# A four-batch vision layer pair on one core: square roots through ln and exp, normalization on ScalarE, weighted sums on TensorE, last stores on another queue

## The chip, the core and the metric

The kernel runs on one core of a Trainium2 chip. The core has five engines with a queue each: PE (TensorE, matrix products), DVE (VectorE), ACT (ScalarE), POOL (GpSimd) and SP (SyncE, which here only issues DMAs). Each engine takes its instructions strictly in the order of its queue; engines wait for each other through semaphores. An instruction that waits holds everything behind it on its engine.

The metric is the device time of one execution in microseconds (us). Before the change it is 4483.56 us, the median of three runs (4473.93 to 4485.39).

## The reference

Input x is 4 batches of 384 channels by 32 x 32 pixels, that is, 1024 tokens of 384 values per batch, all float32. Two layers follow each other:

```
x = x + L0_conv(ln_c(x))        # selective scan in four directions, then layernorm and gelu
t = tokens(x)
t = t + L0_ffn(ln_t(t))         # mixture of 4 experts, the best 2 per token, weighted
x = x + L1_conv(ln_c(x))        # attention, 8 heads of 64, keys = queries = values
t = t + L1_ffn(ln_t(t))         # a feed-forward layer with Kronecker weights, gelu

def _ln_c(v, eps=1e-6):
    return (v - mean(v)) / sqrt(var(v) + eps)

# the experts' part:
probs = softmax(x @ gate_w + gate_b); keep the two largest, divide by their sum -> masked
y_e = gelu(x @ w1[e] + b1[e]) @ w2[e] + b2[e]
out = sum over e of masked[e] * y_e

# the scan's step size, and the scan itself, for each channel and 16 states:
dt = softplus(...) ; h = h * exp(dt * A) + dt * u * B ; y = sum(h * C)
```

Every normalization needs 1/sqrt(var + eps). Each token's result of the expert stage is a sum of two experts' rows, each times a gate weight.

## The kernel before, in words

**Two strands.** The scan (`scan_layer`) takes the four batches one after the other. The tail of a batch (experts, attention, feed-forward) runs beside the scan of the next batches: the tail of batch b-1 is emitted after the scan of batch b in the program, but a planner, which simulates a time for every instruction, sets the order of each engine's queue. Instructions of route, combine, prologue and last_layers have a higher priority. What stands in a queue is therefore the planner's order, and a change of one instruction's cost or engine reorders many others.

**The scan.** A batch has 4 directions x 2 halves of 512 positions x 3 groups of 128 channels = 24 blocks, here called chunks; four batches have 96. A chunk (`chunk`) takes 16 blocks of exp, scan and product: ACT makes `da` = exp(dt * A) (L429) into one of two PSUM buffers; POOL makes `bx` (L420) in one of six buffers; DVE scans (L434, into `bx` or in place into `da`) and multiplies half of the results by C (L441), POOL the other half (L448); PE sums over the states (L455, `acc`), which frees `bx`; DVE adds `acc` to `y` (L282, L286). One chunk ahead, `project` computes dt: ACT's Abs, Relu, Exp (L351), Identity (L352), Ln (L353), Identity, and then DVE's L383 and a copy L384; the result goes to DRAM and comes back spread over partitions (`dtr<-dd`).

**Roots.** `layernorm` (two halves per call; `start` before a batch's scan and `finish` after it) squares on ACT, sums with PE into `ln_var`, takes Sqrt (L178), and a reciprocal on DVE (L180). `stats` (in `prologue` and in `last_layers`) and `spread` (in `route`) do the same with bn_stats, Sqrt (L525, L636) and reciprocal. ACT holds one table set at a time. `exp_again` (L144) puts a load of the set `natural_log_exp_and_others` behind every Sqrt and every Gelu. Where an activation's function is not in the set that is active at its place in the queue, the compiler puts a load ahead of it.

**Experts.** `route` sorts the tokens by expert: it normalizes rows on DVE (L649) and scatters them with 16 indirect DMAs from POOL (L654). `experts` runs 11 slots: xs is gathered, transposed, multiplied by w1 (L879, `h_ps`), bias on ACT (L884), Gelu (L888), multiplied by w2 (L895, `y_ps`), bias added by DVE (L899), and stored to `made` by SP's queue (L900).

**Combine and prologue.** When the last slot is stored, `combine` loads the tokens into `xt`, gathers each token's two rows into `got` (16 indirect DMAs from POOL, L913), scales each by its gate on ACT into PSUM (L920), adds them to `xt` on DVE (L924), and stores `xt` through SP (L925). `prologue` takes the stats of `xt`, normalizes it in place on DVE (`normalize`, L531, which has to wait for that store), transposes with PE (L939, `tc_ps`) and copies with ACT (L943, `xc`). Attention starts with products of `xc` (L964, `w_ps`), then `s_ps` (L987), `ex` (L992), `o_acc` (L1036). `last_layers` is L1083 to L1156, with Gelu at L1128.

route(b+1) is emitted between attention(b) and last_layers(b), so the experts of batch b+1 follow the attention of batch b. The last batch is routed after the scan's end in a larger pool of buffers (`WIDE`).

**Buffers that the change touches.** `k4` (4 KB per partition: 5 buffers, 4 in WIDE) holds xs, xc, y, ex and others; `kw` (8, or 10 in WIDE) holds expert weights, then `got`, then attention's `w`, `vt` and `att`; `w_ps` is two PSUM banks.

Of the kernel before, what the change touches and what calls it, by code (L numbers as in the profile page):

```python
# [12 lines left out]
ALU = mybir.AluOpType  # L13
# [4 lines left out]
P = 128  # L18
# [96 lines left out]
class Body:  # L115
# [29 lines left out]

    def col(self, name, i):
        at = COL[name][0] + i
        return self.cols[:, at : at + 1]

    def layernorm(self, src, dst, eps, psum, work):  # L150

        nc = self.nc
        for i in range(NH):
# [16 lines left out]
            for m in range(nm):  # L170
# [6 lines left out]
            self.exp_again(  # L177
                nc.scalar.activation(std, var[:, :nm], AF.Sqrt, bias=eps, scale=1.0 / D).ins  # L178
            )
            nc.vector.reciprocal(std, std)  # L180
# [304 lines left out]
    def first_layer(self, b, room):  # L485

        self.experts(b, self.slots, room)
        with self.tc.high_priority(offset=FORWARD):
            xt = self.combine(b, *self.place, room)
            return self.prologue(xt, xt, room)  # L490
# [25 lines left out]
    def stats(self, xt, eps, room):  # L516
# [8 lines left out]
        self.exp_again(nc.scalar.activation(rstd, mv[:, :, 1], AF.Sqrt, bias=eps).ins)  # L525
        nc.vector.reciprocal(rstd, rstd)
        return mv[:, :, 0], rstd

    def normalize(self, xt, mean, rstd, out):
        for m in range(MB):  # L530
            self.nc.vector.tensor_scalar(  # L531
                out[:, m, :], xt[:, m, :], mean[:, m : m + 1], rstd[:, m : m + 1],
                op0=ALU.subtract, op1=ALU.mult,
            )
# [71 lines left out]
    def spread(self, b, x1, room):  # L606
# [29 lines left out]
        self.exp_again(nc.scalar.activation(rstd, mv[:, :, 1], AF.Sqrt, bias=self.eps5).ins)  # L636
        nc.vector.reciprocal(rstd, rstd)
        nc.vector.tensor_mul(sc, sc, rstd.unsqueeze(2).to_broadcast([P, MB, NE]))
        nc.vector.tensor_add(sc, sc, self.bg.unsqueeze(1).to_broadcast([P, MB, NE]))
        pos, gate, expert = self.places(sc, room)  # L640
# [4 lines left out]
        for m in range(MB):  # L645
            if m % 2 == 0:
                xt = room.tile([P, 2, D], "k4", "xt")
                nc.sync.dma_start(out=xt, in_=self.tokens(b)[:, m : m + 2, :])
            nc.vector.tensor_scalar(  # L649
                xt[:, m % 2, :], xt[:, m % 2, :], mv[:, m, :1], rstd[:, m : m + 1],  # L650
                op0=ALU.subtract, op1=ALU.mult,
# [155 lines left out]
    def experts(self, b, routed, room):  # L807
# [57 lines left out]
        for s in range(NSLOT):  # L865
# [34 lines left out]
            nc.sync.dma_start(  # L900
# [29 lines left out]
    def prologue(self, xt, xn, room):  # L930

        nc = self.nc
# [453 lines left out]
```

## Time and profile before

| What | us |
|---|---|
| median of three runs | 4483.56 |
| the profiled execution's own time | 4517.48 |
| its span | 4513.6 |
| PE busy | 3440.6 (76%) |
| POOL busy | 3037.0 (67%) |
| DVE busy | 3010.8 (67%) |
| ACT busy | 2534.3 (56%) |
| ACT table loads, 185 of 1283 ns | 237.3 |
| mean granted TensorE clock | 0.831 |

The profile is one execution on the chip. In the lines shown below, "L420" is line 420 of the program, "PEld" the weight loads of PE, and `out<-in` names buffers. A group line gives the engine, the operation, the shapes and the count, then the busy time in us, the mean in ns of one, the idle time of the engine just before these instructions, and what ended that idle time. A line of stretches gives start and end, the length, the busy us of each engine with the count of instructions, the granted clock of PE, the DMA engines' mean busy share and the GB/s. A line of waits names who waited for whom, the total in us, how many times, and the longest. A line of the chain gives a start, a length and what the end of the kernel was waiting for.

PE splits each float32 product into two recorded matmuls, so 912 products of y_ps appear as 1824.

### The profile page before, as it was taken

What the parts mean: (1) busy time and instruction counts of PE and PEld (TensorE: products, weight loads), DVE (VectorE), ACT (ScalarE), POOL (GpSimd) and SP (SyncE); (2) the same over time, 40 slices, a digit from 0 to 9 for tenths busy, and PEclk for the clock granted to TensorE, in tenths of its full rate; (3) what the DMA queues carried; (4) which work ended last, traced back from release to release, by engine and by line L of the source; (5) the groups of instructions that cost most, each with busy time, mean ns of one, the idle gap of its engine ahead of it and who ended that gap; (6) DMA issues with size and microseconds to landing.
All of it is one profiled execution on the core that took longest, in us unless ns stands there. A gap on an engine that the chain in (4) does not pass through costs nothing. (4 is left out here: it accounts for less than half of the span.)

```text
span 4513.6 us, 46925 instructions
## 1 busy us (share of the span) xinstructions
PE 3440.6 (76%) x13852; PEld 1652.0 (37%) x13852; DVE 3010.8 (67%) x4344; ACT 2534.3 (56%) x4406; POOL 3037.0 (67%) x1467
## 2 busy tenths in 40 slices
PE   6545554479894787669998588757998689999796
PEld 2111121145552222225555222214555445556333
DVE  4999997878878977977877777896778520002102
ACT  4555554456665676466666577556666444334554
POOL 4999998788987877778988778878889510000100
PEclk7666665589996898669998699858999789999897
DMA  4444554477886533457779443445787543344200
GB/s 119 118 123 118 146 136 106 137 230 209 231 240 181 149 84 104 130 159 226 210 220 275 137 114 101 115 139 170 232 244 232 169 157 115 107 127 153 75 16 15
DMA packets 404361, 684.81 MB, mean 152 GB/s; under 512 B 50944, under 2 KB 206464, under 8 KB 404096
## 3 DMA queue, kind: packets, MB, share of 16 engines
q1 hardware_dynamic: 395360, 656.16, 50.3%
q0 software_dynamic: 8192, 25.17, 1.7%
q8 instruction: 111, 1.82, 0.2%
q14 instruction: 154, 1.26, 0.1%
q10 hardware_dynamic: 544, 0.40, 0.0%
HBM read 561.47 MB, written 120.06 MB: 151 GB/s over the span
## 5 line engine op out<-in xcount | busy, mean ns | idle before, releaser
L420 POOL TENSOR_TENSOR bx<-dtr,bcs 128x1024 f32<-128x1024 f32 x768 | 1797.8, 2366 | 227.7 <-PE acc L455 103.5
L429 ACT ACTIVATE da<-dtr,nega 128x512 f32<-128x512 f32 x1536 | 1045.5, 691 | 1039.4 <-DVE bx L441 569.0
L448 POOL TENSOR_TENSOR bx<-bx,bcs 128x1024 f32<-128x1024 f32 x384 | 903.6, 2358 | 211.8 <-DVE bx L434 88.0
L455 PE MATMUL acc<-bx,sel 128*32 128x512 f32 x3072 | 511.8, 713 | 312.4 <-POOL bx L448 248.8
L879 PE MATMUL h_ps<-xc,w 128*128 128x256 f32 (+1 forms) x3168 | 680.1, 370 | 61.7 <-DVE xc L861 31.5
L895 PE MATMUL y_ps<-w,hs 128*128 128x384 f32 x1824 | 649.9, 509 | 49.8 <-ACT hs L888 44.1
L879 PEld LDWEIGHTS h_ps<-xc,w 128*128 128x128 f32 x3168 | 557.2, 200 | 253.4 <-issue 120.4
L434 DVE TENSOR_TENSOR_SCAN bx<-da,carry,bx 128x512 f32<-128x512 f32 x384 | 474.0, 1269 | 118.6 <-POOL bx L420 65.5
L434 DVE TENSOR_TENSOR_SCAN bx<-da,bx 128x512 f32<-128x512 f32 x384 | 452.2, 1209 | 129.2 <-POOL bx L420 70.3
L434 DVE TENSOR_TENSOR_SCAN da<-da,carry,bx 128x512 f32<-128x512 f32 x384 | 476.5, 1273 | 67.9 <-ACT da L429 62.6
L441 DVE TENSOR_TENSOR bx<-da,bcs 128x512 f32<-128x512 f32 x768 | 509.8, 679 | 3.8
L434 DVE TENSOR_TENSOR_SCAN da<-da,bx 128x512 f32<-128x512 f32 x384 | 456.3, 1218 | 60.7 <-ACT da L429 44.2
L895 PEld LDWEIGHTS y_ps<-w,hs 128*128 128x128 f32 x1824 | 352.3, 198 | 341.7 <-issue 86.4
L992 ACT ACTIVATE ex<-s_ps 128x512 f32<-128x512 f32 x512 | 299.4, 591 | 274.9 <-PE s_ps L987 259.9
L987 PE MATMUL s_ps<-w 64*128 64x512 f32 x1024 | 308.4, 674 | 83.1 <-ACT ex L992 74.2
L1077 POOL TENSOR_TENSOR xt<-xt,wb 128x3072 f32<-128x3072 f32 x4 | 26.8, 6708 | 477.5 <-DMA w<-in_w 345.5
L1036 PE MATMUL o_acc<-ex,vt 128*64 128x512 f32 x1024 | 295.6, 658 | 0.8 <-ACT att L1044 0.8
L455 PEld LDWEIGHTS acc<-bx,sel 128*32 128x32 f32 x3072 | 77.7, 117 | 596.0 <-POOL bx L448 363.8
L884 ACT ACTIVATE hs<-h_ps,bb 128x256 f32<-128x256 f32 (+1 forms) x528 | 194.0, 447 | 128.8 <-PE h_ps L879 128.5
L899 DVE TENSOR_TENSOR y<-y_ps,bb 128x384 f32<-128x384 f32 x76 | 41.6, 548 | 237.6 <-PE y_ps L895 237.6
L913 POOL DMA_INDIRECT got<-made,g_pos x64 | 60.8, 950 | 192.4 <-PE f_acc L1136 159.1
L987 PEld LDWEIGHTS s_ps<-w 64*128 64x128 f32 x1024 | 81.1, 192 | 266.8 <-ACT ex L992 149.1
(216 smaller groups left out, 4021.9 us busy)
## 6 DMA issues: line engine op xcount, KB each, us to landing
w<-in_w SPq DMA_DIRECT2D x352, 576.0 KB
dtr<-dd SPq DMA_DIRECT2D x1536, 128.0 KB
bcs<-rows SPq DMA_DIRECT2D x512, 128.0 KB
dd<-one_e SPq DMA_DIRECT2D x96, 256.0 KB
dd<-mag SPq DMA_DIRECT2D x96, 256.0 KB
rows<-zero SPq DMA_DIRECT2D x76, 192.0 KB
xs<-rows SPq DMA_DIRECT2D x32, 384.0 KB
made<-y SPq DMA_DIRECT2D x32, 384.0 KB
```

The costliest lines, as they stand in the source:

```text
L420: pool = nc.gpsimd.tensor_mul(bx, dtr[q][1], bc[:, 0].unsqueeze(1).to_broadcast([P, 2, HF])).ins
L429: nc.scalar.activation(da, dtr[q][0][:, j, :], AF.Exp, scale=nega[:, col : col + 1])
L434: nc.vector.tensor_tensor_scan(run(h), run(da), run(bx[:, j, :]), 0.0 if first else hold, ALU.mult, ALU.add,)
L441: dve = nc.vector.tensor_mul(bx[:, j, :], h, cg).ins
L448: pool = nc.gpsimd.tensor_mul(bx, bx, cg.unsqueeze(1).to_broadcast([P, 2, HF])).ins
L455: nc.tensor.matmul(acc[lo : lo + DB, :], sel, out[q][:, j, :], start=(g == 0), stop=(g == NG - 1),)
L879: nc.tensor.matmul(ps[:, r, :], w1[(f + r) // wf][:, c, (f + r) % wf * P : ((f + r) % wf + 1) * P], xc[:, c, :], start=(c == 0), stop=(c = ...
L884: nc.scalar.activation(hs[:, f + r, :], ps[:, r, :], AF.Identity, bias=bb[:, f + r : f + r + 1])
L895: nc.tensor.matmul(out[:, :D], hs[:, f, t * P : (t + 1) * P], w2[f // wf][:, f % wf, :], start=(f == 0), stop=(f == FC - 1),)
L987: nc.tensor.matmul(ps[:, o, :], w[rows, j * P : (j + 1) * P], w[rows, halves(i)], start=True, stop=True,)
L992: ins = nc.scalar.activation(ex[:, o, :], ps[:, o, :], AF.Exp, scale=HD**-0.5, accum_out=sums[:, t, 2 * j + o, i : i + 1],).ins
L1036: ins = nc.tensor.matmul(out[cols, :], made[t][1][:, j, cols], ex[:, o, :], start=(j == 0), stop=(j == MB - 1),).ins
```

## The change

It has four parts.

1. `inverse_root` replaces Sqrt, `exp_again` and reciprocal at three places (layernorm, stats, spread): Ln of the variance plus eps, then Exp of -0.5 times that, both on ACT. `exp_again` stays behind the Gelus.
2. `normalize` (DVE) is gone. `less_mean` computes -mean * rstd in one small DVE product; ACT then computes x * rstd + less with one Identity per 128 rows, in `prologue` and in `spread`. In `prologue`, after `combine`, the result goes into the first half of `got` instead of into `xt`.
3. `combine` no longer scales on ACT and adds twice on DVE. POOL multiplies the identity matrix by each gate column into `diag`, two tiles of 128 x 1024, ahead of the gathers; PE multiplies these diagonal matrices with the gathered rows and sums the two experts in PSUM; DVE adds two groups of 128 tokens at a time.
4. The store of the last slot of each batch is issued from ACT's queue, the other ten still from SP's.

```diff
+    def inverse_root(self, out, var, eps, scale=1.0):
+        self.nc.scalar.activation(out, var, AF.Ln, bias=eps, scale=scale)
+        self.nc.scalar.activation(out, out, AF.Exp, scale=-0.5)
...
-            self.exp_again(
-                nc.scalar.activation(std, var[:, :nm], AF.Sqrt, bias=eps, scale=1.0 / D).ins
-            )
-            nc.vector.reciprocal(std, std)
+            self.inverse_root(std, var[:, :nm], eps, scale=1.0 / D)
...
-        self.exp_again(nc.scalar.activation(rstd, mv[:, :, 1], AF.Sqrt, bias=eps).ins)
-        nc.vector.reciprocal(rstd, rstd)
+        self.inverse_root(rstd, mv[:, :, 1], eps)
...
-    def normalize(self, xt, mean, rstd, out):
-        for m in range(MB):
-            self.nc.vector.tensor_scalar(
-                out[:, m, :], xt[:, m, :], mean[:, m : m + 1], rstd[:, m : m + 1],
-                op0=ALU.subtract, op1=ALU.mult,
-            )
+    def less_mean(self, mean, rstd, room, tag):
+        less = room.tile([P, MB], tag, "less")
+        self.nc.vector.scalar_tensor_tensor(less, mean, -1.0, rstd, op0=ALU.mult, op1=ALU.mult)
+        return less
...
-            nc.vector.tensor_scalar(
-                xt[:, m % 2, :], xt[:, m % 2, :], mv[:, m, :1], rstd[:, m : m + 1],
-                op0=ALU.subtract, op1=ALU.mult,
+            nc.scalar.activation(
+                xt[:, m % 2, :], xt[:, m % 2, :], AF.Identity,
+                bias=less[:, m : m + 1], scale=rstd[:, m : m + 1],
             )
...
-            nc.sync.dma_start(
+            queue = nc.sync if s + 1 < NSLOT else nc.scalar
+            queue.dma_start(
                 out=made[at : at + size, :].rearrange("(t p) d -> p t d", p=P), in_=y
             )
...
+        diag = []
+        for k in range(TOP):
+            d = room.tile([P, MB, P], "k4", "diag")
+            nc.gpsimd.tensor_mul(
+                d, self.ident.unsqueeze(1).to_broadcast([P, MB, P]),
+                gate[:, k, :].unsqueeze(2).to_broadcast([P, MB, P]),
+            )
+            diag.append(d)
...
-        for m in range(MB):
+        for m in range(0, MB, 2):
             ps = room.two("w_ps")
-            for k in range(TOP):
-                nc.scalar.activation(
-                    ps[:, k, :D], got[m][:, k, :], AF.Copy, scale=gate[:, k, m : m + 1]
-                )
-            for k in range(TOP):
-                nc.vector.tensor_add(xt[:, m, :], xt[:, m, :], ps[:, k, :D])
+            for o in range(2):
+                for k in range(TOP):
+                    nc.tensor.matmul(
+                        ps[:, o, :D], diag[k][:, m + o, :], got[m + o][:, k, :],
+                        start=(k == 0), stop=(k == TOP - 1),
+                    )
+            nc.vector.tensor_add(xt[:, m : m + 2, :], xt[:, m : m + 2, :], ps[:, :, :D])
         nc.sync.dma_start(out=self.tokens(b), in_=xt)
-        return xt
+        return xt, [got[m][:, 0, :] for m in range(MB)]
...
-        self.normalize(xt, mean, rstd, xn)
+        less = self.less_mean(mean, rstd, room, "less")
+        for m in range(MB):
+            nc.scalar.activation(
+                xn[m], xt[:, m, :], AF.Identity, bias=less[:, m : m + 1], scale=rstd[:, m : m + 1]
+            )
```

A third path, `second_layer_exact`, which runs only if a sum overflows, is adapted to the new arguments; it is not executed with these inputs.

More of the change, by code (lines that the diff above doesn't have):

```diff
@@ L488, in first_layer @@
         with self.tc.high_priority(offset=FORWARD):
-            xt = self.combine(b, *self.place, room)
-            return self.prologue(xt, xt, room)
+            xt, xn = self.combine(b, *self.place, room)
+            return self.prologue(xt, xn, room)
     def second_layer(self, b, xc, room, between):
@@ L635, in spread @@
             nc.sync.dma_start(out=self.tokens(b)[:, m : m + 2, :], in_=xt)
-        self.exp_again(nc.scalar.activation(rstd, mv[:, :, 1], AF.Sqrt, bias=self.eps5).ins)
-        nc.vector.reciprocal(rstd, rstd)
+        self.inverse_root(rstd, mv[:, :, 1], self.eps5)
         nc.vector.tensor_mul(sc, sc, rstd.unsqueeze(2).to_broadcast([P, MB, NE]))
         nc.vector.tensor_add(sc, sc, self.bg.unsqueeze(1).to_broadcast([P, MB, NE]))
+        less = self.less_mean(mv[:, :, 0], rstd, room, "r_less")
         pos, gate, expert = self.places(sc, room)
@@ L939, in prologue @@
                 nc.tensor.transpose(
-                    ps[:, m // 4, m % 4 * P : (m % 4 + 1) * P], xn[:, m, c * P : (c + 1) * P],
+                    ps[:, m // 4, m % 4 * P : (m % 4 + 1) * P], xn[m][:, c * P : (c + 1) * P],
                     self.ident,
@@ L1179, in second_layer_exact @@
                     nc.sync.dma_start(out=xt, in_=self.tokens(b))
-                    nc.vector.tensor_copy(xc, self.prologue(xt, xt, room))
+                    xn = [xt[:, m, :] for m in range(MB)]
+                    nc.vector.tensor_copy(xc, self.prologue(xt, xn, room))
                 with ExitStack() as part:
```

## The prediction

> **What bounds the kernel now.** I read the 40 slices first, then stretches between marks found in the timeline, then waits, then the chain. In the slices each digit is a tenth of busy time:
>
> ```profile
> PE   6545554479894787669998588757998689999796
> DVE  4999997878878977977877777896778520002102
> POOL 4999998788987877778988778878889510000100
> ```
>
> POOL and DVE are full while the first batch is scanned (slices 2 to 6), high together with PE while scans and tails overlap, and idle at the end, where only PE is busy. The kernel has three limits. The stretches show them (columns: length; busy us of PE, PEld, DVE, ACT, POOL; clock; DMA):
>
> ```profile
> 91.00:652.00 561.00, 300.57 (x894) 75.84 (x893) 516.77 (x700) 301.14 (x471) 554.31 (x241) 0.67 0.50 129
> 841.00:900.00 59.00, 18.28 (x38) 3.11 (x38) 58.64 (x113) 18.12 (x28) 39.63 (x19) 0.50 0.44 119
> 1399.00:1459.00 60.00, 11.41 (x41) 4.17 (x42) 52.19 (x69) 27.13 (x43) 48.88 (x33) 0.51 0.52 146
> 3546.00:3622.00 76.00, 41.71 (x155) 31.35 (x154) 31.49 (x72) 31.71 (x42) 22.56 (x22) 0.59 0.42 132
> 3622.00:3692.00 70.00, 56.06 (x221) 19.50 (x219) 17.29 (x87) 31.79 (x87) 15.42 (x16) 0.90 0.64 220
> 3692.00:4185.00 493.00, 478.44 (x1973) 281.87 (x1971) 46.07 (x79) 190.02 (x385) 6.68 (x1) 0.98 0.37 118
> 4185.00:4247.00 62.00, 35.62 (x178) 19.62 (x177) 19.49 (x43) 33.65 (x39) 15.20 (x16) 0.73 0.41 130
> 4247.00:4513.00 266.00, 231.51 (x996) 85.14 (x994) 29.55 (x56) 133.58 (x314) 6.69 (x1) 0.90 0.05 15
> ```
>
> Row 1 is 20 of the scan's 96 chunks, 28.05 us each: POOL is busy 99%, DVE 92%. Row 2 is the chunk under route(0), all DVE; row 3 the one under combine(0), DVE and POOL. Both take 60 us. The scan ends at 3546; from there PE is idle 34 + 14 + 15 + 26 + 35 = 124 us of 968. DVE's waits in row 1 (total us, times, longest):
>
> ```profile
> DVE bx L434 <- ACT da L429: 10.6, 49, 1.2
> DVE y L286 <- PE acc L455: 8.9, 9, 1.9
> DVE da L434 <- ACT da L429: 8.7, 7, 2.0
> DVE bx L434 <- POOL bx L420: 5.4, 6, 1.7
> ```
>
> **Part A: table loads in the first batch.** The before-kernel executes 185 loads:
>
> ```profile
> L144 ACT ACT_TABLE_LOAD x92 | 118.0, 1283 | 1.6
> L178 ACT ACT_TABLE_LOAD x16 | 20.5, 1283 | 4.8 <-PE ln_var L172 4.6
> L525 ACT ACT_TABLE_LOAD x8 | 10.3, 1283 | 0.1
> L636 ACT ACT_TABLE_LOAD x4 | 5.1, 1283 | 0.1
> ```
>
> 28 Sqrt (16 + 8 + 4) cost a load and a load back: 56. The change drops them, and with them the hint after each that chose the one set with both ln and exp. In the order of the built program nothing chooses that set until the first Gelu, after batch 0. Until then Ln takes one set and Exp another: 27 loads ahead of project's Ln, 27 behind, 12 in layernorm, where there were 12 in all. That is 54 x 1.283 = 69 us more ACT in batch 0, and 195 loads instead of 185.
>
> Who is late: each chunk has one Ln, so ACT loses 2 x 1.283 = 2.57 us per chunk, with DVE's next da queued behind. Matching the n-th da exp with the n-th scan in the timeline, the exp behind an Ln ends only 0.29 us ahead of its scan (mean of 24), so 2.28 us reach DVE. DVE's own chunk is 516.77/20 = 25.84 busy + 0.97 waiting for da + 0.21 for dt_ps = 27.02; its other waits are POOL's doing. POOL's 28.05 hides 1.03. Loss: 24 x (2.28 - 1.03) = 30 us. At the start, where nothing hides it, each of two layernorm halves has load 1.283 + Exp 0.23 for reciprocal 0.17, and the first Ln a load: 2 x 1.34 + 1.28 = 4. I take **+34**; bounds: 4 (POOL's lead of up to six bx buffers hides the rest) and 4 + 69 = 73. No gain is possible here.
>
> The Trainium skill ("ScalarE: Activation LUTs", Table sets) has ln followed by exp as one load, since one set holds both; by that A would be about 0 and the sum lower by 34. The trace agrees as long as that set is active (Exp, Identity, Ln of project follow each other at 0.63 us with no load); the order as built does not keep it. The same page (What ACT_TABLE_LOAD costs) adds a drain of 1380 ns to a load of 1283; with it 69 would be 144. The rows have the load at 1283, with idle of 0.1 us before L525's eight.
>
> **Part B: inside the scan, batches 1 to 3.**
> B1, loads gone: 15 roots before 3546 (eight layernorm halves, four stats, three routes) free 2.57 us of ACT each, 38.5. POOL, DVE and PE take turns as the limit there (83%, 81%, 79% of 1000:3000), so I count under half: **-16** (0 to -38).
> B2, DVE work: L531 (32 x 0.791), L649 (32 x 1.009) and 64 adds L924 x 0.551 go, 16 adds of 128x768 come (nearest row L1087, 0.948): -78; reciprocals (28 x 0.17) against 12 small products cancel to -3. ACT loses 64 copies L920 and gains 64 Identity of the same shape, 0.584 each: zero. Where DVE sets the stretch, this counts: route(0) has 11.9 us of L649, I take -10; combine(0) has 12.0 of L531 and 8.9 of adds, -8, because 16 gathers (L913, 0.95 + 0.30 each) hold POOL 20 us anyway; combine(1), route(1), route(2) -3 each (DVE 60 to 70% busy). **-27** (0 to -60).
> B3, diag on POOL: two products of 128x1024 per batch (nearest L420, 2.37), ahead of the gathers; combine(0) and (1): **+9** (0 to 9.5). For batch 3 POOL has waited 159 us and hides it.
> B4, diag matmuls: 16 per batch. L895, the same 128x384, does 12 in 9.70 us: 0.81 each, 13 us. They keep the pace of the gathers, but PE is in order: acc L455 behind them, which frees bx for POOL, waits until the last gather lands, 3.1 us after its issue, plus 0.8: **+8** for two (0 to 20).
> B5, last store: ACT waits for DVE's y add, with da exps queued behind. DVE makes that add itself and ACT leads it by two da at most: 2 us each, **+6** for three (0 to 20).
> B sums to **-20**.
>
> **Part C: the tail's chain.** From the last y add to the first w_ps of attention the four batches take 70, 95, 68 and 63 us (timeline). The new chain: store to first gather 3.0 + 16 issues 19.7 + landing 3.1 + two matmuls 1.6 + add 0.95 + two stats 1.5 + Ln, Exp, product 1.0 + eight Identity 4.7 + remaining transposes and three copies 5.5 = 41. What goes, in batch 3 (start, us, what):
>
> ```profile
> 4222.59 2.77 ACT hs L1128
> 4232.67 5.66 DMA x<-xt
> 4238.43 3.21 DVE xt L531 x8
> ```
>
> Gelus of last_layers no longer stand between ACT's copies, and the normalized rows go into got, so they don't wait for xt's store. In batch 1 the y store stood 16 us behind others on SP's queue; on ACT's it doesn't. experts(b+1) follow attention(b), so by combine(2) the tail is 29 + 54 = 83 us further ahead of the scan; the built order agrees, with combine(2) two chunks before the scan's end (before: after it).
>
> After the scan's end: attention(2) fills PE while layernorm, route(3) and its scatters run (146 us before, 138 with three roots less). PE work moved ahead of it: the last y 7, transposes 6, projections 10, an eighth of attention(2) 18 = 41; 13 comes for diag. Busy: 843 - 41 + 13 = 815. Idle: about 12 in the first stretch (was 48), 15, 22 under combine(3) (41 less diag 13 and transposes 6), 34 at the end: 83. 815 + 83 = 898 instead of 968: -70. last_layers(2), about 31 us of PE, no longer fills combine(3)'s wait; that is in the busy sum. Paid back: combine(2)'s gathers and diag, 19.7 + 4.7 of POOL, now lie inside the scan: +20 (its four-fifths busy share). **-50** (from -70 to +20).
>
> **Sum:** +34 - 20 - 50 = -36. The profiled execution took 4517.48 (span 4513.6), 34 above the median 4483.56; I set the difference against the median: **4448**. Singly, 12 us is about what this kernel's runs differ by; 0.3% is 13.5.
>
> The skill's page also says (Rules for kernel authors) to use VectorE, not ScalarE, for adds and products. Uncontended, L531's eight take 3.21 us and eight at L920's rate 4.67, so the rule would cost 1.5 us in batches 2 and 3; under the scan L531 took 12.0 and the rows are against it.
>
> **Rivals.**
> 1. POOL's lead hides the loads (A = 4): 4 - 20 - 50, **4418**. For it: POOL 99% busy. Against: DVE 92%, 1.03 us of slack.
> 2. The loads count in full (A = 73): +3, **4487**, no change. For it: lead of 0.1 us at the median Ln. Against: POOL's 1.03.
> 3. Slower: the lead is paid back. combine(2) inside the scan holds POOL and PE, the scan ends 20 later, and nothing after it gets shorter, because PE serves acc and finish first: 34 - 20 + 20 = +34, **4518**. It decides (slower by over 13.5) if the stretch after the scan shortens by less than 20, not 70. For it: PE is 91% busy over 3300:3540. Against: 48 us of PE idle in 3546:3692.
>
> **How the numbers follow.** Forecast 0.42 (own range 4425 to 4470), rival 1 0.13, rival 2 0.13, rival 3 0.24, and 0.08 for several bounds at once beyond 4525, since a planner reorders all queues. Faster 0.42 + 0.13 = 0.55, same 0.13, slower 0.24 + 0.08 = 0.32. Range 4405 to 4525: about 0.1 left out on each side.
>
> **What would show it.** A: 66 loads before the first Gelu, chunks of batch 0 at 29.3 instead of 28.05 us, DVE waiting for da some 45 us more in 91:652. B: the 60 us chunk of route(0) near 50. C: about 41 us from last y to w_ps, stretch after the scan near 898. The forecast is wrong if batch 0's chunks stay at 28.05, or if that stretch stays over 948.

## The result, and the profile after

The changed kernel took 4534.85 us (median of four runs, 4528.43 to 4536.92). The kernel before, on the same runs, took 4478.75 (four runs). The ratio is **1.0122, 95% interval [1.0102, 1.0143]**: 56 us slower, where 36 us faster was forecast. The time lies above the predicted range. The kernel before, unchanged, took 4511, 4481, 4520 and 4512 us in four later sets of runs, the first two of them on one chip; the cause is open, and kernels are compared within a set of runs unless a comparison across sets is called that.

The first view of the changed kernel's page, the 40 slices:

```profile
PE   5554554549997888669998788759998688999796
DVE  4888888778887866978877776888887720020002
POOL 3899988778998867788888787878898810000100
```

In slices 2 to 6 (the first batch) DVE is at 8 instead of 9, and POOL drops to 8 twice: something else holds them back. After the scan PE's row looks like before; a slice of 113 us is too coarse for what changed there, and the stretches have to show it.

The same stretches as in the prediction, between the marks of the changed kernel (length; busy us of PE, PEld, DVE, ACT, POOL; clock; DMA):

```profile
97.00:699.00 602.00, 307.78 (x900) 76.97 (x898) 518.87 (x702) 354.06 (x511) 554.44 (x241) 0.67 0.43 121
890.00:942.00 52.00, 21.63 (x72) 7.00 (x64) 50.88 (x112) 23.12 (x39) 40.77 (x20) 0.53 0.42 126
1446.00:1519.00 73.00, 49.04 (x164) 18.74 (x165) 58.66 (x62) 36.32 (x70) 55.62 (x31) 0.81 0.56 155
3626.00:3772.00 146.00, 117.89 (x530) 49.66 (x531) 31.07 (x115) 63.63 (x169) 23.20 (x23) 0.87 0.37 129
3772.00:4225.00 453.00, 432.31 (x1841) 270.33 (x1839) 42.77 (x71) 178.04 (x312) 10.50 (x3) 0.98 0.41 131
4225.00:4267.00 42.00, 23.21 (x57) 10.87 (x58) 9.04 (x22) 7.43 (x12) 15.22 (x16) 0.74 0.49 155
4267.00:4530.00 263.00, 232.76 (x995) 85.07 (x994) 29.53 (x55) 131.22 (x313) 6.70 (x1) 0.90 0.04 14
```

Row 1 is the same 20 chunks of batch 0: 602 us instead of 561, 30.1 a chunk instead of 28.05, with the same work on DVE (519 against 517) and POOL (554 both) and 53 us more on ACT. Row 2, the chunk of route(0), fell from 59 to 52. Row 3, the chunk that holds the rest of combine(0) and the prologue, is 73 us long. The last four rows are the stretch after the scan: 904 us where it was 967 between the same marks.

The costliest table loads of the changed kernel (groups by line; count, busy us, mean ns, idle time before):

```profile
L144 ACT ACT_TABLE_LOAD x64 | 82.1, 1283 | 1.2
L355 ACT ACT_TABLE_LOAD x27 | 34.6, 1283 | 4.2 <-DMA dd<-one_e 3.2 <-PE dt_ps L360 0.5
L431 ACT ACT_TABLE_LOAD x25 | 32.1, 1283 | 0.4
L148 ACT ACT_TABLE_LOAD x6 | 7.7, 1283 | 4.4 <-PE ln_var L177 4.3
L149 ACT ACT_TABLE_LOAD x6 | 7.7, 1283 | 0.1
L353 ACT ACT_TABLE_LOAD x2 | 2.6, 1283 | 0.0
```

L355 is `project`'s Ln, L431 the exp of `da`, L148 and L149 the new Ln and Exp, L353 `project`'s Exp: 27 + 25 + 6 + 6 + 2 = 66 loads. Of these, 62 lie in batch 0; with one more (L208) that the kernel before has too, batch 0 has 63 loads where it had nine. Here is one pair in ACT's timeline (start, us):

```profile
123.14 0.63 ACT L354 ACTIVATE one_e<-mag 128x512 f32<-128x512 f32 x1
124.52 1.28 ACT L355 ACT_TABLE_LOAD   x1
125.82 0.63 ACT L355 ACTIVATE lnw<-one_e 128x512 f32<-128x512 f32 x1
126.47 1.28 ACT L431 ACT_TABLE_LOAD   x1
127.76 0.69 ACT L431 ACTIVATE da<-dtr,nega 128x512 f32<-128x512 f32 x1
```

One Ln between exps costs a load there and a load back, once a chunk. DVE's waits in row 1's stretch (total us, times, longest) say who pays:

```profile
DVE bx L436 <- ACT da L431: 47.3, 59, 2.9
DVE da L436 <- ACT da L431: 20.5, 12, 4.0
DVE bx L436 <- POOL bx L422: 6.4, 4, 2.8
DVE y L288 <- PE acc L457: 5.7, 9, 1.3
```

The waits for `da` are 67.8 us; they were 19.3. All others together fell only from 24.1 to 17.2.

### The profile page after: what moved, and what is told of

Its sections match the earlier page's. It is cut to its first block, busy times and chain, and to the rows that moved or that the text cites. A ratio compares the mean times of both kernels' runs of the same rounds, so it can differ in the third digit from the quotient of the medians.

```text
span 4535.1 us, 47114 instructions
## 1 busy us (share of the span) xinstructions
PE 3477.0 (77%) x13980; PEld 1651.3 (36%) x13980; DVE 2963.0 (65%) x4212; ACT 2553.7 (56%) x4444; POOL 3053.6 (67%) x1475
## 5 line engine op out<-in xcount | busy, mean ns | idle before, releaser
L431 ACT ACTIVATE da<-dtr,nega 128x512 f32<-128x512 f32 x1536 | 1044.4, 690 | 1016.7 <-DVE bx L443 596.7
L457 PE MATMUL acc<-bx,sel 128*32 128x512 f32 x3072 | 521.7, 707 | 295.5 <-POOL bx L450 249.1
L916 POOL TENSOR_TENSOR diag<-ident,g_picked 128x1024 f32<-128x1024 f32 x8 | 15.0, 1893 | 262.8 <-PE xc_ps L858 249.6
L347 PE MATMUL dt_ps<-xd,wdt 12*128 12x512 f32 x192 | 127.8, 751 | 68.7 <-ACT mag L386 49.7
```

Source lines behind the costliest of these rows:

```text
L431: nc.scalar.activation(da, dtr[q][0][:, j, :], AF.Exp, scale=nega[:, col : col + 1])
L457: nc.tensor.matmul(acc[lo : lo + DB, :], sel, out[q][:, j, :], start=(g == 0), stop=(g == NG - 1),)
```

## The experiments

There are sixteen runs in four further sets, each beside the kernel before. "Stages" are read from each trace by the last scan of a batch: batch 0 / batches 1 to 3 / after the scan.

| Kernel | us, median | ratio to before, 95% | stages of its profile |
|---|---|---|---|
| *set 1: before* | 4510.83 | | |
| e0, before, one run | 4516.03 | | 750 / 2801 / 960 |
| e1, change + one load at the start | 4487.02 | 0.9947 [0.9935, 0.996] | 747 / 2821 / 911 |
| e2, part 1 alone | 4594.43 | 1.018 [1.015, 1.021] | 808 / 2811 / 975 |
| e3, part 1 + one load at the start | 4537.68 | 1.0058 [1.0035, 1.0081] | 749 / 2808 / 976 |
| *set 2: before* | 4480.51 | | |
| e4, e1 without part 4 | 4480.66 | 0.9999 [0.9987, 1.0011] | 750 / 2851 / 879 |
| e5, e1 without part 3 | 4488.17 | 1.0021 [1.0005, 1.0037] | 750 / 2822 / 908 |
| e6, e1 without part 2 | 4495.58 | 1.0042 [1.0022, 1.0062] | 751 / 2814 / 926 |
| e7, the change again | 4532.12 | 1.0113 [1.0096, 1.013] | 806 / 2833 / 904 |
| *set 3: before* | 4520.33 | | |
| e8, before, one run | 4518.05 | | 750 / 2801 / 964 |
| e9, e1 again | 4493.78 | 0.9944 [0.9931, 0.9958] | 750 / 2845 / 912 |
| e10, e1 + product on ACT | 4491.99 | 0.9944 [0.993, 0.9957] | 750 / 2814 / 919 |
| e11, e10 + diag on ACT | 4482.21 | 0.9911 [0.9895, 0.9926] | 751 / 2813 / 917 |
| *set 4: before* | 4511.77 | | |
| e12, before, one run | 4508.96 | | 750 / 2794 / 961 |
| e13, the change a third time | 4552.89 | 1.0096 [1.0078, 1.0113] | 807 / 2828 / 908 |
| e14, e11 again | 4468.51 | 0.9906 [0.9892, 0.9919] | 749 / 2795 / 920 |
| e15, e1 a third time | 4485.26 | 0.9944 [0.9927, 0.9962] | 747 / 2824 / 911 |

**How large the change's own cost is: e0, e7, e8, e12, e13.** These are the two kernels unchanged.

e0_before_again:

> The kernel before, unchanged, for a second profile. Its first profiled execution took 4517.48 us, 34 more than the median of its other runs, and the scan's batches ended at 748, 1686, 2631 and 3547. Theory 1 (that execution was an unusual one): the profiled time is near 4480 and one of the stretches is shorter by some 34. Theory 2 (profiling costs this kernel 34 us, though it costs the changed one nothing): again near 4517, with the same ends within 5 us.

e7_after_again:

> The changed kernel, unchanged, timed beside the kernel before and beside the three kernels that follow. Two sets of runs had the kernel before at 4479 and at 4511 us, so the set of runs matters by 0.7%. Theory 1 (the loads of batch 0 cost the same in every set): 57 to 65 us above the same kernel with a load at the start, which had a ratio of 0.9947 to before: a ratio of 1.007 to 1.010. Theory 2 (the kernel before alone depends on the set of runs): about 4535 us again, a ratio near 1.005.

e8_before_look:

> The kernel before, unchanged, beside the runs of the kernel before in this set. Its median was 4479 and 4481 us in two sets of runs and 4511 in a third, and the profile of before that the prediction was worked out from (4517) belongs to the third kind. If this set is of the first kind (4475 to 4490), theory 1 (chance waits of VectorE for GpSimd, spread over the scan) expects the 30 us in the batch ends, 748, 1686, 2631, 3546 us in the profile shown, each batch a little earlier; theory 2 (memory placement of the experts' weights) expects the batch ends as shown and the stretch after the scan (960 us) some 30 shorter. If this set is of the other kind, both expect 4510 to 4525 and nothing is learned.

e12_before_third:

> The kernel before, unchanged, one profile. If this set is of the faster kind (median of before 4475 to 4490), chance waits expect earlier batch ends than 748, 1686, 2631, 3546 us, a little in each batch; a placement of the weights in memory expects those batch ends and a stretch after the scan of about 930 instead of 960 us. If it is of the slower kind (4505 to 4525): the batch ends of the profile shown, and nothing more.

e13_after_third:

> The changed kernel, unchanged. It took 4535 and 4532 us where the kernel before took 4479 and 4481. In a set of the slower kind: if the set moves only the kernel before, 4530 to 4540 again, a ratio of 1.003 to 1.006, and the change's own cost is the 22 us of the two profiles; if it moves both, 4562 to 4572, 1.011 to 1.013, and the profiles mislead. In a set of the faster kind: 4530 to 4537, 1.010 to 1.014, as before.

The ratio came out at 1.0122, 1.0113 and 1.0096 in three sets, so the slowdown is the change's own. The changed kernel moves with the set too (4532 and 4535 where the kernel before takes 4480, 4553 where it takes 4512), though less. e0 came out at the number of its theory 2, but not for its reason: the other runs of that set took 4511, so profiling doesn't cost 34 us. e8 and e12 could not decide between their theories. e7 lies just above the ratio of its theory 1, and e13 between its two forecasts. The profile of before that the prediction worked from (4517) and that of the changed kernel shown above (4537) show 19 us of the 56 when laid side by side. Set 4 gives a pair from one set. Stretches by stage, the kernel before (e12):

```profile
0.00:750.00 750.00, 406.51 (x1210) 121.50 (x1210) 633.15 (x859) 391.23 (x607) 670.10 (x307) 0.67 0.48 124
750.00:3544.00 2794.00, 2195.28 (x9128) 1097.13 (x9129) 2231.48 (x3150) 1722.68 (x2935) 2301.01 (x1105) 0.85 0.61 178
3544.00:4505.00 961.00, 837.21 (x3515) 433.01 (x3513) 144.38 (x337) 420.79 (x864) 66.56 (x56) 0.92 0.31 100
```

and the changed kernel (e13):

```profile
0.00:807.00 807.00, 414.25 (x1218) 120.09 (x1218) 633.59 (x855) 462.50 (x665) 674.84 (x309) 0.67 0.41 116
807.00:3635.00 2828.00, 2263.42 (x9344) 1116.23 (x9341) 2205.23 (x3096) 1710.23 (x2972) 2323.78 (x1125) 0.87 0.59 178
3635.00:4542.80 907.80, 803.12 (x3423) 414.63 (x3423) 113.44 (x263) 381.87 (x809) 56.74 (x43) 0.93 0.30 98
```

Batch 0 +57, batches 1 to 3 +34, after the scan -53: +38 by spans, +41 by the medians. By batch, the middle stage is 934, 942 and 918 us in e12 and 934, 963 and 931 in e13: the loss lies in batches 2 and 3. In PE's column 34 us of work left the last stage, and 68 came into the middle one; 47 of these 68 are the new products with the diagonal matrices (96 of 128 run there). No profile of the kernel before was taken in a set in which it takes 4480, so in which stage those 30 us lie stayed open.

**What the table loads of batch 0 cost: e1, e2, e3, e9, e15.** e2 is the kernel before with part 1 alone; e1 is the changed kernel, and e3 is e2, with one line at the start of the program:

```diff
+        with tc.high_priority():
+            nc.scalar.preload_act_table_set("natural_log_exp_and_others")
         self.ident = ...
```

e1_preload:

> The changed kernel with one load of the table set that holds ln and exp at the very start, so that the 66 loads before the first Gelu become 1. Theory 1 (those loads cost batch 0 the 57 us by which it ends later, 805 against 748, and the delay is carried to the end): batch 0 ends near 748 again, its chunks near 28.05 us, and the time falls by about 57 to 4478, no change against the kernel before. Theory 2 (POOL hides the loads and the reordered queues cost the time): batch 0 gets shorter, but the time stays above 4515. The planner sees one more instruction, so later queues may be reordered: 20 us either way.

e2_roots:

> The kernel before with part 1 of the change alone (Ln and Exp for Sqrt and reciprocal), without a load at the start: 195 loads, 66 of them before the first Gelu, as in the changed kernel. Theory 1 (loads of batch 0 are the cost): batch 0 ends near 805, and the time is 4478 + 57 less up to 38 for the 44 loads saved later: 4497 to 4535. Theory 2 (the cost lies in parts 2 to 4): within 15 us of 4478.

e3_roots_preload:

> The kernel before with part 1 alone and with one load of the set with ln and exp at the start: 129 loads instead of 185, none between Ln and Exp. Theory 1: batch 0 ends near 745 and the 44 loads saved later are worth 0 to 38, so 4440 to 4478. Theory 2 (later loads don't matter and the planner's order does): anywhere within 20 us of 4478.

e9_preload_again:

> The changed kernel with the one table load at the start, once more, so that it and the next two are compared with the kernel before on the same runs. It took 4487 us where the kernel before took 4511 (0.9947). If the set of runs moves the kernel before alone, it takes 4480 to 4492 again, a ratio of 0.999 to 1.003 where the kernel before takes 4480; if the set moves both, it takes 4450 to 4465 there, 0.994 to 0.997.

e15_preload_third:

> The changed kernel with one table load at the start, beside the changed kernel itself on the same runs. The theory that the loads of batch 0 are carried in full to the end expects it 45 to 60 us below e13 (the batch ended 58 us earlier: 747 instead of 805); a rival in which later waits swallow part of them, 15 to 35 below.

The one load, from e15's groups, is the only one in its batch 0:

```profile
L126 ACT ACT_TABLE_LOAD x1 | 1.3, 1283 | 0.8 <-PEq L1398 0.8
```

and DVE's waits in the same 20 chunks of e15 are those of the kernel before:

```profile
DVE bx L438 <- ACT da L433: 10.5, 48, 1.2
DVE da L438 <- ACT da L433: 8.9, 8, 2.0
```

e2 - e3 is 57 us (four runs each), e13 - e15 is 68 (six runs each, 61 by the two profiles), a little above the 45 to 60 forecast. e1's batch 0 is back at 747, as forecast; that it would also beat the kernel before was not forecast. In both pairs batch 0 ends 59 to 60 us earlier and the later stages differ by under 5 us: what batch 0 loses is carried to the end in full. With the one load the changed kernel (e1, e9, e15) beats the kernel before, by 0.53 to 0.56% in three sets. In all three the kernel before took 4511 to 4520; how the two compare where it takes 4480 was not run.

Two forecasts missed. e2 lies 84 us above the kernel before, where 19 to 57 was forecast. And e3 lies 27 above it, where it was to be faster or within 20. It executes 129 loads instead of 185 and one DVE instruction fewer per root, and is still 0.6% slower than the kernel before. Its middle stage is 7 to 14 us longer, and its last stage 15. Freed ACT time in batches 1 to 3 bought nothing there. That the planner's order has put route(1) and all behind it some 20 us later is what the trace shows; whether this order is the cause was not tested.

**What each other part is worth: e4, e5, e6.** All three start from e1. e4 puts the last store back on SP's queue, e5 takes back the scaling by ACT and the adds by DVE, e6 the normalization on DVE (into `got`, as in the change):

```diff
 e4
-            queue = nc.sync if s + 1 < NSLOT else nc.scalar
+            queue = nc.sync
 e5
-        diag = []
...
-                    nc.tensor.matmul(
-                        ps[:, o, :D], diag[k][:, m + o, :], got[m + o][:, k, :],
-                        start=(k == 0), stop=(k == TOP - 1),
-                    )
...
+            for k in range(TOP):
+                nc.scalar.activation(
+                    ps[:, k, :D], got[m][:, k, :], AF.Copy, scale=gate[:, k, m : m + 1]
+                )
+            for k in range(TOP):
+                nc.vector.tensor_add(xt[:, m, :], xt[:, m, :], ps[:, k, :D])
 e6, in prologue; in spread alike
-            nc.scalar.activation(
-                xn[m], xt[:, m, :], AF.Identity, bias=less[:, m : m + 1], scale=rstd[:, m : m + 1]
-            )
+            nc.vector.tensor_scalar(
+                xn[m], xt[:, m, :], mean[:, m : m + 1], rstd[:, m : m + 1],
+                op0=ALU.subtract, op1=ALU.mult,
+            )
```

e4_store_sp:

> The changed kernel with a load at the start and without part 4: the last stores are issued from SP again. Theory 1 (the move only spares batch 1 a wait of 16 us on SP's queue, under the scan): within 8 us of the kernel with a load at the start (ratio 0.9947), and y to w_ps of batch 1 some 16 us longer than its 67.6. Theory 2 (ACT waiting for y costs the scan): faster by 6 to 20.

e5_combine_act:

> The changed kernel with a load at the start and without part 3: ACT scales the rows, DVE adds them, no diag. Theory 1 (the chain of the tail is what the change shortens): from the last y to w_ps of batch 3 about 50 to 60 us instead of 42, 10 to 30 us slower than with part 3. Theory 2 (PE held for the gathers and diag on POOL cost the scan as much): within 8 us.

e6_norm_dve:

> The changed kernel with a load at the start and without part 2: DVE normalizes again, 64 instructions of 128x384, but into the rows of got. Theory 1 (DVE's time in the chunks under route and combine counts): 10 to 25 us slower, and the chunk of route(0) near 60 instead of 52 us. Theory 2 (those stretches are POOL's): within 8 us.

e1 itself was not in this set. Against the changed kernel on the same runs (e7) the three are 51, 44 and 37 us faster by the medians, and 63, 63 and 52 by the profiled spans; e15, with all parts, is 68 and 61 faster than e13. So, across sets, the store is worth 17 or nothing, the sums on TensorE 24 or nothing, the normalization on ScalarE 31 or 10, and the two ways of reading differ by more than the effect: what is shown is that undoing no single part brings back a missing gain. The expected sizes of e4 to e6 as shares of e1 can't be judged closer than that. Of what was expected inside the traces, three things missed. Batch 1's chain in e4 did not get 16 us longer: it takes 63 us, 68 in e1. Batch 3's chain in e5 stayed at 42 instead of 50 to 60. And route(0)'s chunk in e6 went back to 56, not to 60.

They also say what shortened the tail's chain in batch 3. From the last y add to the first w_ps it takes 63.1 us in e12, 61.0 in e3, and 41.7, 41.8 and 39.8 in e4, e5 and e6. So part 1 alone does not do it, and the store, the sums and ScalarE's normalization are none of them needed for it. What e4, e5 and e6 share, and e3 lacks, is that the rows go into `got` instead of back into `xt`; each also keeps two of parts 2 to 4, so that any two of these might do it was not ruled out. In e3's timeline, DVE's normalization still waits for the store of `xt`:

```profile
4250.38 0.38 SPq L927 DMA_DIRECT2D x<-xt  x1
...
4256.14 3.20 DVE L534 TENSOR_SCALAR xt<-xt,mv,rstd 128x384 f32<-128x384 f32 x8 [4.97 <-DMA x<-xt]
```

That is 5 of the 20 us. The rest is order. In e3, ACT's part of that chain has the Gelu of last_layers(2) with its two loads inside it:

```profile
4240.83 1.28 ACT L1130 ACT_TABLE_LOAD   x1
4242.12 2.76 ACT L1130 ACTIVATE hs<-hs 128x3072 f32<-128x3072 f32 x1
4244.90 1.28 ACT L146 ACT_TABLE_LOAD   x1
```

e5, with the same scaling by ACT, has nothing of last_layers there and needs 7 us from the last gather to the first transpose, where e3 needs 27. Whether the `got` tile alone makes the planner choose that order was not tried by itself.

**Where batches 1 to 3 might get longer: e10, e11, e14.** The changed kernel's chunk of combine(0) led to one small instruction. Its DVE and POOL timelines:

```profile
1461.68 12.25 DVE L533 SCALAR_TENSOR_TENSOR less<-mv,rstd 128x8 f32<-128x8 f32 x1 [0.61 <-ACT rstd L149]
1473.86 2.45 DVE L436 TENSOR_TENSOR_SCAN bx<-da,carry,bx 128x512 f32<-128x512 f32 x2
...
1458.85 9.24 POOL L422 TENSOR_TENSOR bx<-dtr,bcs 128x1024 f32<-128x1024 f32 x4
1468.06 1.25 POOL L378 TENSOR_TENSOR lnw<-lnw,mag 128x512 f32<-128x512 f32 x1
1469.28 4.62 POOL L422 TENSOR_TENSOR bx<-dtr,bcs 128x1024 f32<-128x1024 f32 x2
1476.45 2.35 POOL L450 TENSOR_TENSOR bx<-bx,bcs 128x1024 f32<-128x1024 f32 x1 [2.54 <-DVE bx L436]
```

A product of eight numbers per partition takes 12.25 us, and 0.17 in batch 3. It ends (1473.93) when POOL's unbroken run of products ends (1473.90). PE's transposes and DVE's scans stand behind it, and then POOL in turn has to wait 2.54 us for DVE. Over the kernel (groups of the changed kernel; `inv`, attention's row factor, is a small DVE sum of the same kind, whose two inputs lie in SBUF as well):

```profile
L533 DVE SCALAR_TENSOR_TENSOR less<-mv,rstd 128x8 f32<-128x8 f32 x8 | 37.6, 4695 | 1.8 <-ACT rstd L149 1.8
L916 POOL TENSOR_TENSOR diag<-ident,g_picked 128x1024 f32<-128x1024 f32 x8 | 15.0, 1893 | 262.8 <-PE xc_ps L858 249.6 <-DMA made<-y 13.2
L1018 DVE TENSOR_TENSOR inv<-sums 128x16 f32<-128x16 f32 x16 | 11.0, 685 | 198.5 <-ACT ex L1010 198.5
```

The kernel before has such holds too, which the prediction did not see. Its own views show them, as `inv` and as one row of the old normalization (count, then ns min/median/max, then the first and last start):

```profile
L1000 DVE TENSOR_TENSOR inv<-sums 128x16 f32<-128x16 f32 x16 | 30.4, 1900 | 214.7 <-ACT ex L992 214.7
L531 DVE TENSOR_SCALAR xt<-xt,mv,rstd x32: 453/472/8690, 1443.5 to 4241.2; 128x384 f32<-128x384 f32 x32
```

The row of 8.69 us is the first of combine(0), and it ends 0.22 us after a POOL product does. In the changed kernel the product of L533 stands in its place. In the pair of set 4, `less` and `inv` together take 38.7 us in e13, and `inv` alone 31.2 in e12: the holds are moved more than they are added.

e10 takes this product off DVE; e11 and e14 take the diagonal matrices off POOL as well:

```diff
 e10, in less_mean
-        self.nc.vector.scalar_tensor_tensor(less, mean, -1.0, rstd, op0=ALU.mult, op1=ALU.mult)
+        minus = room.tile([P, MB], tag + "_m", "minus")
+        self.nc.scalar.activation(minus, mean, AF.Copy, scale=-1.0)
+        for m in range(MB):
+            self.nc.scalar.activation(
+                less[:, m : m + 1], minus[:, m : m + 1], AF.Copy, scale=rstd[:, m : m + 1]
+            )
 e11 and e14, also in combine
-            nc.gpsimd.tensor_mul(
-                d, self.ident.unsqueeze(1).to_broadcast([P, MB, P]),
-                gate[:, k, :].unsqueeze(2).to_broadcast([P, MB, P]),
-            )
+            for m in range(MB):
+                nc.scalar.activation(
+                    d[:, m, :], self.ident, AF.Copy, scale=gate[:, k, m : m + 1]
+                )
```

e10_less_act:

> The same kernel, with the product -mean*rstd (128x8) on ScalarE in nine small instructions instead of one on VectorE. In the profile of the changed kernel VectorE's product lasts 0.15 to 12.75 us, 37.6 in all eight, and its long ones end within 0.03 us of the end of one of GpSimd's products. Theory (the port: VectorE is held until GpSimd pauses, the scan behind it, and GpSimd then waits for buffers in turn): the chunk of combine(0) falls from 72 us to 60 to 64, that of combine(1) from 70 to 60 to 64, route(0)'s stays at 52, batches 1 to 3 together take 15 to 30 us less than the 2821 of the kernel beside it, and the time is 15 to 30 us lower. Rival (TensorE held for the gathers, or the built order, make these chunks long, and VectorE would wait there anyway): the chunks stay at 68 to 74, the time within 6 us of the kernel beside it. If the chains of the tail are what counts, the extra 1.6 us of ScalarE in each of the seven products cost up to 5 us after the scan.

e11_less_diag_act:

> The kernel with that product on ScalarE, and the diagonal matrices too: 16 copies of 128x128 a batch on ScalarE with the gates as scale, instead of two products of 128x1024 on GpSimd (1.9 us each on average, 2.4 under the scan). Theory B3 (4.7 us of GpSimd count in full in combine(0) and combine(1)): 5 to 10 us below the kernel with the product alone moved. Rival (they run while GpSimd waits for the last store in any case, or ScalarE's 16 copies of some 0.25 us delay the exps of da by as much): within 5 us of it, or up to 5 above.

e14_best_again:

> The changed kernel with one table load at the start, the product -mean*rstd and the diagonal matrices on ScalarE, once more: 4482 us in a set where the kernel before took 4520 (0.9911). If it gains by itself, 4470 to 4485 again, that is 0.990 to 0.993 of a before at 4511 to 4520, or 0.997 to 1.001 of one at 4480; 6 to 14 below the kernel with the single load in either case.

e10 is half a hit. The chunks of combine(0) and combine(1) fall to 56 and 58 us, below the 60 to 64 forecast, but the time does not follow: 4491.99 against 4493.78, where 15 to 30 less was forecast. The chunk behind that of combine(1) takes 65 us, where it took 33 in e9. And another hold is longer:

```profile
L1025 DVE TENSOR_TENSOR inv<-sums 128x16 f32<-128x16 f32 x16 | 42.1, 2630 | 199.9 <-ACT ex L1017 199.9
```

`inv` took 11.0 in the changed kernel and 12.3 in e15, and takes 42.1 here. That is not simply the hold of L533 passed on, for e4 has both long (39.8 and 40.6): which small instruction meets a run of POOL products changes with the order of the queues. By the medians the product alone is worth nothing (0.9944 both). The pair's profiles, 31 us apart in batches 1 to 3, can't be set against that, since e9's profiled execution took 4508.84, 15 above its median.

With the diagonal matrices moved too, e11 lies 9.8 us below e10 by the medians of five runs each. B3 had +9 for them. But the middle stages of the two profiles are 2814 and 2813 us, and POOL's products took 1.88 to 1.91 us in all eight cases of the changed kernel, not 2.37, so that the gain comes by B3's way is not shown. Both moves together give 11.6 and 16.7 us (e11 against e9, e14 against e15; 6 to 14 was forecast for e14). **e14 is the version that beats both kernels**: 0.9911 [0.9895, 0.9926] and 0.9906 [0.9892, 0.9919] of the kernel before, 84 us below the changed kernel on the same runs (4468.51 against 4552.89). Both of these sets had the kernel before at 4512 to 4520. ACT is busy 19.1 us with the 64 copies of the identity (0.39 each, overlapping) where POOL paid 15.0, and POOL is the fuller engine.

## Why the prediction failed, step by step

Set against the pair from one set (e12, e13):

| Term of the sum | predicted | found |
|---|---|---|
| A, batch 0 | +34 | +57 |
| B with the 20 paid back by combine(2), batches 1 to 3 | 0 | +34 |
| C, stretch after the scan | -70 | -53 |
| sum | -36 | +38 |

**A: right mechanism, wrong size.** 66 loads came, at the lines named; DVE's wait for `da` in the 20 chunks grew by 48.5 us where 45 was forecast. The step that failed is "POOL's 28.05 hides 1.03". It assumed that DVE's other waits vanish once DVE is late. The rows of the other waits sum to 24.1 us before (8.9 + 5.4 + 4.2 + 3.6 + 2.0) and still to 17.2 after (6.4 + 5.7 + 2.9 + 2.0 + 0.2): 0.35 a chunk was hidden, not 1.03. POOL's own waits in the 20 chunks show why. They were 6.4 us in all in the kernel before and are 47.4 in the changed one, these among them:

```profile
POOL bx L450 <- DVE carry L447: 18.8, 6, 6.3
POOL bx L450 <- DVE bx L436: 9.7, 3, 5.5
POOL bx L422 <- PE acc L457: 6.5, 3, 3.1
```

POOL multiplies half of what DVE has scanned. When exp is late, the scan and the carry behind it are late, and POOL waits for them: 28.5 us, where it was 2.0. The wait for `acc` doubled as well, from 3.2 to 6.5. So POOL's pace was not a floor under DVE; it follows DVE. Chunks took 30.1 us instead of the 29.3 forecast; 20 chunks cost 41, the last three of the batch 10, the start 6.

By the Trainium skill ("ScalarE: Activation LUTs", Table sets) ln followed by exp needs one load. The runs show that this depends on which set is already active: 63 loads in batch 0 without the line at the start, one with it. The drain of 1380 ns that the same page (What ACT_TABLE_LOAD costs) adds to each load isn't seen: Ln follows its load at 125.82, 0.02 us after it, and 54 loads more in batch 0 cost 57 us there (e13 against e12), about 1.06 us each.

**B: the gain was not there.** Its terms, as far as the runs reach:
- B1 (-16): counted under half of the freed ACT time. e3 frees it, and its middle stage is 7 longer than e0's. No gain is seen there.
- B2 (-27): route(0)'s chunk fell to 52 (near 50 forecast), but with the rows normalized on DVE (e6) batches 1 to 3 take 2814 us, with them on ACT 2821 to 2845 (across sets). DVE time freed in one chunk does not shorten the three batches; what e6 loses lies after the scan (926 against 911). The term was also mis-read: of the 12.0 us that it took for L531 in combine(0), 8.69 are one row held beside POOL's products, where the median row takes 0.47. That is no work that a move to ACT takes away, and in the changed kernel L533 is held there, for 12.25 us.
- "Reciprocals against 12 small products cancel to -3" counted twelve products where eight were built, and had them at some 0.17 each: L533 takes 37.6 us (26.5 in e13). But e10 shows that moving them alone brings nothing, so this is not simply the missing 34.
- B3 (+9): e11's 9.8 has its size; that it has its place is not shown. B4 and B5 were not singled out; e5 and e4 only show that the parts that bring them cost nothing clear on balance.

So the step of B that failed is the claim that DVE and ACT time taken out of batches 1 to 3 shortens them (-16 and -27). What made them 34 us longer instead stays open. PE's work does not set their length: e5, which lacks the products with the diagonal matrices, has 47 us less of it there than e1 and the same length (first row e1, second e5, third e14):

```profile
747.00:3568.00 2821.00, 2255.25 (x9347) 1116.93 (x9347) 2207.63 (x3096) 1704.30 (x2967) 2323.92 (x1126) 0.87 0.60 178
750.00:3572.00 2822.00, 2207.79 (x9175) 1096.70 (x9175) 2230.97 (x3132) 1724.04 (x2987) 2313.00 (x1120) 0.85 0.59 178
749.00:3545.00 2796.00, 2225.30 (x9253) 1101.37 (x9255) 2191.55 (x3091) 1717.40 (x3039) 2311.58 (x1120) 0.87 0.61 179
```

Two readings are left. One is the tail's lead: the prediction had combine(2) alone pay 20 for it, and all the tail work pulled under the scan may cost more. e4 fits that, with the longest middle stage (2851) and the shortest last one (879). The other is the work on DVE and POOL that e14 moves to ACT. In set 4 e14's middle stage is 2795 us, 2824 in e15 and 2794 in the kernel before, and 41 of the 53 us gained after the scan are still there. But combine(2) starts only 35 us ahead of the scan's end in e14, 89 in e13 and e15, so the lead is smaller too. No run varied the lead by itself: neither reading is shown.

**C: the steps held in batch 3, the term was a quarter too large.** Last y to first w_ps in batch 3 took 41.9 us (41 forecast). In batches 0 to 2, under the scan, it took 50, 67 and 55. In the kernel before the same reading gives 60, 91 and 62, not the 70, 95 and 68 of the prediction, so the chain gave 10 + 24 us of the lead by combine(2), not 29 + 54. "The rule would cost 1.5 us" has its sign reversed: DVE's eight rows at 3.21 us are 1.5 shorter than ACT's at 4.67, and the chain of e6, with DVE normalizing, is 2 us shorter than e5's (39.8 against 41.8). The chain in ACT's timeline of the changed kernel reads as forecast, with L533 at 0.17 because POOL is idle there:

```profile
4225.14 0.33 ACTq L902 DMA_DIRECT2D made<-y  x1
4254.79 0.30 ACT L148 ACTIVATE rstd<-mv,eps 128x8 f32<-128x8 f32 x1 [38.53 <-DVE mv L526]
4255.61 4.89 ACT L950 ACTIVATE got<-xt,less,rstd 128x384 f32<-128x384 f32 x8 [0.28 <-DVE less L533]
```

The stretch after the scan is 904 to 910 us (898 forecast). In the rows above, PE is busy 806 us of it (815 forecast) and idle 98 (83): the idle of the first stretch fell from 48 to 28, not to 12; 15.2 us of that is one wait for the gather of `xs`, and 11.8 is `s_ps` of attention(2) waiting for ACT's `ex`. The other 7 us are in the starting value, 968 in the profile that was used and 961 in e12's.

**The rivals.** The outcome is none of the three. Rival 2 had the loads near their upper bound, which was right, but B and C unchanged. Rival 3 had the right sign by the wrong mechanism: the stretch after the scan did shorten. POOL's lead (rival 1) hid a third of a microsecond a chunk. What was left out was that A near its upper bound and B at a loss come together; the 0.08 given to several bounds at once was too little, since both rest on one assumption, that time freed or slack beside a full engine can be spent.

**The base.** "I set the difference against the median" took the 34 us between profile and median for chance. The later profiles of the kernel before (4516, 4518 and 4509) each lie within 6 us of the median of their own set (4511, 4520 and 4512), so most likely the 34 us are a difference between sets of runs; the changed kernel has some 20 of it (4553 against 4532 and 4535).

## What to carry to other kernels

Dropping the instruction that switched a table also drops the hint that chose the right one: count loads per stage in the built order, and set the table once, ahead of the first use, when a single set serves all. Slack next to an engine that is busy 99% isn't a cushion when that engine works on what the late one hands it: here 0.35 us a chunk of 2.4 were hidden, so count a new delay per round nearly in full unless a row shows the other engine running rounds ahead. And freed time on engines that take turns as the limit bought nothing in e3 and e10: ask first for a wait in that very stretch that names it. Before pricing a row by its mean, look at its median: a long one among short ones may be a wait, and it can pass to the next instruction.

## What was not expected of the hardware

- A small DVE product with both inputs in SBUF can stand still while POOL runs products back to back. L533 lasted 0.15 to 0.17 us in the three cases in which no POOL product went on beside it, 2.35 and 2.36 in two cases, and 7.36, 12.25 and 12.75 in three; each of these five ended within 0.03 us of the end of a POOL product. In the three longest POOL's run had ended; in the two of 2.35 and 2.36 it went on at once, so DVE can also get through between two products. `inv` shows the same holds (15.01 in the kernel before). The scans, with one input in PSUM, keep to 1.15 to 1.31 us over the whole kernel.
- The Trainium skill ("SBUF — State Buffer", SBUF: two separate sides, Who interferes with whom) says that the two engines share a port pair under an exclusive lock, held for one whole instruction, and that a DVE instruction with two SBUF inputs competes for it. The trace agrees on who is held. It differs on how long: if the lock changed hands after each instruction, at most about one POOL product, 2.35 us, where 12.75 were measured, five products and a half-size one in a row.
